# Two graph layers on one core: copies of values and transposes moved to ScalarE, the second graph's queries in seven products, and a rearranged beginning

## The chip, the cores and the metric

The kernel runs on one core of a Trainium2 chip. The core has a matrix engine (TensorE, PE in the profile, its weight loads apart as PEld), a vector engine (VectorE, DVE), a scalar engine (ScalarE, ACT), a general engine (GpSimd, POOL) and a sync engine (SP) that here only issues transfers. Each works through its own list of instructions in order and waits for the others by semaphores. The metric is the device time of one execution, in microseconds.

## What is computed

x has 16 graphs of 1024 nodes with 256 features. Both layers are residual and begin with a layer norm and a relu.

```python
h = jnp.maximum(_layernorm(x), 0.0)          # layer 0
c_adj = mean of h over its features
diff  = c_adj[:, None, :] - c_adj[:, :, None]
A     = abs(abs(sigmoid(diff) - 0.5) - 0.5) * 2.0
Wg    = adj * (A + A^T) / 2                  # one 1024 x 1024 matrix for each graph
g     = relu((h^T @ Wg) * para)              # the queries, 4 heads of 64
k, v  = h @ kv_w
x     = x + softmax(q k^T * scale) v
...
h = jnp.maximum(_layernorm(x), 0.0)          # layer 1
x = x + batchnorm(relu(batchnorm(A_hat @ h @ W1^T + b1)) @ W2^T + b2)
```

A_hat is the normalized adjacency with the identity added, the same for all graphs. All of it is float32.

## The kernel before

**Stages.** `layers` runs graph after graph. While the attention of graph b is computed, a "background" works on its neighbours: keys, values and queries of graph b+1, the second layer's aggregation and first product of graph b-1, and the norm and transposes of graph b+2. When all graphs are through, `second` does the two batch norms and the last product. A second pass (`shifted`) exists for extreme inputs and isn't entered here.

**Attention.** A unit is one graph, one pair of heads and one half of the queries; a graph has four units of four steps, and a step takes two of the eight key tiles. `scores` (L874) issues two score products per step into PSUM and two exponentials (L890, ACT). `Unit.values` (L914) multiplies the exponentials of the step before with v. `Unit.add` sums them on DVE (L909, L912), and the row sums and the outputs are folded in later (L934 to L999).

**The order of the work** is written out by hand in `attention` (L1000). In each step come, in this order: the scores and exponentials, at a "top" the transposes if one is due, the DVE sums, the value products of the step before, and then as many pieces of the background as their costs (1.71 for about 1.9 us of PE) allow against a due sum that grows evenly over the steps. `background` (L786) names the pieces; `weave` (L148) takes a piece of a main stream and then one of each side stream, from the index at which the side starts; `double` takes two of a side at once; `soon` puts an action after the next piece. Each engine executes its instructions in the order in which they were issued here, so a copy that is issued behind an exponential on the same engine waits for it.

**Around the change.**

- `transposed` (L385): for one feature half k, eight transposes on PE into two PSUM banks, and one copy for each bank into `ht` (L399, DVE). In `prepare` (L772) it is called at a top, twice for a graph.
- `keys_values` (L613): four products for the keys, each copied by ACT (L624), and then four groups for the values, `pv`, each with two copies of 128 x 256 into `v` (L641, DVE).
- `bank` (L164): PSUM tiles for all these products come from one pool of two buffers. A third product can't begin before the first has been copied out.
- `queries` (L478): the product h^T Wg in seven block products of half size instead of eight, with sums and differences of blocks on DVE (L512 among them) and two copies on ACT (L515, L516). `plain_queries` (L579): the same product in 32 tile products. In the kernel before, graphs 0 and 1 use the plain form, the others the seven products.
- `weigh` (L419): the matrix Wg in eight tiles `w`: absolute differences (L450) and a tanh (L458) on ACT, and a product with adj on DVE (L437). It reads csum as a row, `cbc`, which for all graphs but the first goes through DRAM (L414, L415). Its pieces are called slots, 17 for a graph.
- `Norm` (L298): statistics on DVE, the inverse root on POOL, the relu on ACT (L341).
- `degrees` (L224) and `graph` (L243): the node degrees, on ACT and DVE, and the combined blocks of the transposed adjacency, on POOL and by transfers issued by POOL. Both run once, in the background of graph 0.
- `aggregate` (L646): the second layer's aggregation, `pa`, in seven products; `hidden` (L721): the product with W1, `py`, whose bias is added by ACT (L737) with a column of `vec`.
- The beginning (L1082 to L1104): norm of graph 0, transposes, keys and values, weighing, plain queries, then `attention`.

Of the kernel before, what the change touches and what calls it, by code (L numbers as in the profile page):

```python
# [17 lines left out]
P = 128  # L18
# [5 lines left out]
def gnn_two_layers_kernel(  # L24
# [12 lines left out]
    nc = tc.nc  # L37
# [19 lines left out]
    neg_half = const.tile([P, NT], F32, name="neg_half")  # L57
    nc.gpsimd.memset(neg_half, -0.5)
    vec = const.tile([P, 18], F32, name="vec")
    nc.sync.dma_start(out=vec, in_=vecs)  # L60
    b1, g1, be1 = (vec[:, i * HC : (i + 1) * HC] for i in range(3))
    b2, g2, be2 = (vec[:, 3 * HC + i * CC : 3 * HC + (i + 1) * CC] for i in range(3))
    stats1 = const.tile([P, HC, B * NH, 6], F32, name="stats1")
# [32 lines left out]
    def layers(shifted):  # L96
# [73 lines left out]
                r = slice(e * HW, (e + 1) * HW)  # L170
                nc.tensor.matmul(dst[r], left[:, r], right, start=start, stop=stop)  # L171

        def load_x(b):
            xs[b] = p3.tile([P, NT, C], F32, tag="x", name=f"x_{b}")
            for half in range(2):
                t = slice(half * NT // 2, (half + 1) * NT // 2)
                nc.sync.dma_start(
                    out=xs[b][:, t], in_=x[b].rearrange("(t p) c -> p t c", p=P)[:, t]
                )
# [8 lines left out]
            )  # L188
            return t

        load_x(0)
        kvw = const.tile([P, CC, 2 * C], F32, tag="kvw", name=f"kvw_{kind}")
        nc.sync.dma_start(out=kvw, in_=kv_w.rearrange("(k p) j -> p k j", p=P))
        rows = big.tile([P, NH, NT], F32, name="rows")
# [190 lines left out]
        def transposed(b, k, halves=range(NH)):  # L385

            h = hs["a", b]
            if 0 in halves:
                ht = p3.tile([P, N], F32, tag="ht", name=f"ht_{b}_{k}")
                hts.setdefault(b, []).append(ht)  # L390
            ht = hts[b][k]
            for g in halves:
                pt = bank(f"htp_{b}_{k}_{g}")
                for j in range(FB // P):
                    t = g * (FB // P) + j
                    nc.tensor.transpose(
                        pt[:, j * P : (j + 1) * P], h[:, t, k * P : (k + 1) * P], ident
                    )
                nc.vector.tensor_copy(ht[:, g * FB : (g + 1) * FB], pt)  # L399

        def differences(b):


            cbc = p1.tile([P, N], F32, tag="cbc", name=f"cbc_{b}")
            cbcs[b] = (
                cbc.rearrange("p (t q) -> p t q", t=NT)
                if b == 0
                else cbc.rearrange("p (q t) -> p t q", t=NT)
            )
            weighers[b] = weigh(b)  # L410
            if b == 0:
                broadcast_row(cbc, columns_of(csums[b], f"c{b}"), f"c{b}")
                return
            nc.sync.dma_start(out=csum_d[b].rearrange("(p t) -> p t", p=P), in_=csums[b])  # L414
            nc.sync.dma_start(  # L415
                out=cbc, in_=csum_d[b].rearrange("(o n) -> o n", o=1).to_broadcast([P, N])
            )
# [195 lines left out]
        def keys_values(b):  # L613
            ht = hts[b]
            ks[b] = [p4.tile([P, N], F32, tag="k", name=f"k_{b}_{k}") for k in range(CC)]
            for g in range(NH):
                for j in range(CC):
                    cols = slice(g * FB, (g + 1) * FB)
                    pk = bank(f"pk_{b}_{j}_{g}")
                    for k in range(CC):  # L620
                        product(
                            pk, kvw[:, k, j * P : (j + 1) * P], ht[k][:, cols], k == 0, k == CC - 1
                        )
                    nc.scalar.copy(ks[b][j][:, cols], pk)  # L624
                    yield 1.71

            vs[b] = [p4.tile([P, NT, P], F32, tag="v", name=f"v_{b}_{k}") for k in range(CC)]
            for g in range(NT // 2):
                pv = bank(f"pv_{b}_{g}").rearrange("p (j c) -> p j c", j=2)
                for j in range(2):  # L630
                    t = 2 * g + j
                    for k in range(CC):
                        product(
                            pv[:, j, :],
                            ht[k][:, t * P : (t + 1) * P],
                            kvw[:, k, C : 2 * C],
                            k == 0,
                            k == CC - 1,
                        )
                for k in range(CC):  # L640
                    nc.vector.tensor_copy(  # L641
                        vs[b][k][:, 2 * g : 2 * g + 2, :], pv[:, :, k * P : (k + 1) * P]
                    )
                yield 1.71
# [141 lines left out]
        def background(b):  # L786

            if b == 0:
                differences(1)
                for k in range(CC):  # L790
                    yield TOP
                    transposed(1, k)
                    yield 1.0
                w, products, norm = weighers[1], keys_values(1), Norm(2, True).all()
                yield from weave(
                    islice(products, 4), (0, double(islice(w, 8))), (0, islice(norm, 4))
                )
                yield from weave(
                    plain_queries(1), (0, norm), (0, w), (5, graph()), (7, degrees())
                )  # L800
                differences(2)
                yield from islice(products, 2)
                yield from prepare(2, products)
                return
            before = hidden(b - 1)
            gather = aggregate(b - 1)
            if b + 1 < B:
                w, products, norm = weighers[b + 1], keys_values(b + 1), normed(b - 1)
                yield from weave(islice(products, 4), (0, islice(w, 4)))
                if b == 1:  # L810
                    load_later()
                yield from weave(queries(b + 1), (0, double(w)), (9, islice(norm, 5)))
                yield next(gather)
                yield from weave(products, (0, norm))
            else:
                yield from weave(endings.pop(), (2, normed(b - 1)))
                yield next(gather)
            if b + 2 < B:
                yield from weave(gather, (3, summed(b + 2)))
                yield from prepare(b + 2, before)  # L820
            elif b + 2 == B:

                yield from gather
                endings.append(before)
            else:
                yield from gather
                yield from weave(before, (0, normed_last()))
# [230 lines left out]
        with st:  # L1058
            if shifted:
                for b in range(B):  # L1060
                    if b > 0:
                        load_x(b)
                    run(Norm(b, True).all())
                    differences(b)
                    for k in range(CC):
                        transposed(b, k)
                    run(islice(weighers[b], AHEAD))
                    run(weave(plain_queries(b), (0, weighers[b])))
                    if b == 0:
                        run(degrees(), graph())  # L1070
                        load_later()
                    run(keys_values(b))
                    shifted_attention(b)
                    norm = Norm(b, False)
                    run(norm.all())
                    nc.gpsimd.dma_start(out=x1_d[b], in_=xs[b])
                    if b == B - 1:
                        attn.close()
                        turns.append(second(kind))
                    run(aggregate(b), hidden(b))  # L1080
            else:
                norm = Norm(0, True)  # L1082
                norm.stats(0, 1)
                norm.scale(0, 2)
                for t in range(2, NT, 2):
                    norm.stats(t, t + 1)
                    norm.shift(t - 2, 2)
                    norm.relu(t - 2, t - 1)
                    norm.scale(t, 2)
                norm.shift(NT - 2, 2)  # L1090
                norm.relu(NT - 2, NT - 1)
                products = keys_values(0)

                for k in range(CC):
                    transposed(0, k, (0,))
                run(islice(products, 2))
                for k in range(CC):
                    transposed(0, k, (1,))
                differences(0)
                run(weave(products, (0, islice(weighers[0], AHEAD))))  # L1100
                load_x(1)
                load_x(2)
                run(weave(plain_queries(0), (0, weighers[0]), (5, Norm(1, True).all())))
                attention()  # L1104
                attn.close()
                turns.append(second(kind))
                run(aggregate(B - 1), hidden(B - 1))
# [324 lines left out]
```

## Time and profile before

| | |
|---|---|
| median of three runs | 2658.61 us (2658.59 to 2659.17) |
| the profiled execution | 2658.52 us |
| its span in the trace | 2656.6 us |
| mean granted clock of TensorE | 0.981 |
| PE busy | 2550.8 us, 96% |
| DVE busy | 1904.3 us, 72% |
| ACT busy | 1402.4 us, 53% |
| POOL busy | 391.4 us, 15% |
| first transpose on PE | at 8.57 us |
| first scores of the attention | at 61.34 us |

The rows of the profile that belong to the two moved copies are `v<-pv` (L641, 128 copies of 418 ns) and `ht<-htp` (L399, 64 copies of 681 ns by their medians). A copy of 128 x 512 from PSUM by ACT (L624) has a median of 585 ns. A row of the timeline gives the start, the length, the engine, the line, the operation, its output and inputs, the count, and in square brackets how long the engine had been idle and what ended that. "Busy" of PE counts modelled ends of pipelined matmuls: two matmuls of half the array's width run beside each other, so that one lasts 592 ns while the group takes 0.22 us for each.

### The profile page before, as it was taken

The page shows a single profiled execution, that of the slowest core. Times are in us where ns is not written, and L with a number is a line of the kernel's source. Part 1 is how long each engine was busy: PE and PEld are TensorE (multiplying, and loading weights), DVE is VectorE, ACT ScalarE, POOL GpSimd, SP SyncE. Part 2 cuts the span into 40 slices and gives each one's busy share as a digit, 9 for nine tenths or more (in the row PEclk, how much of TensorE's full clock was granted, in tenths as well). Part 3 has the DMA queues.
Part 4 walks back from the last instruction along what each step waited for, and adds up shares of the span by engine and source line. Part 5 has one row for each costly group of instructions (what it writes and reads, how often), then busy time and mean ns, then how long its engine had stood idle before and what let it go on. Part 6 is the DMA issues. An engine that isn't in the chain of part 4 may idle for free.

```text
span 2656.6 us, 31371 instructions
## 1 busy us (share of the span) xinstructions
PE 2550.8 (96%) x11626; PEld 948.2 (36%) x11626; DVE 1904.3 (72%) x3029; ACT 1402.4 (53%) x1841; POOL 391.4 (15%) x456
## 2 busy tenths in 40 slices
PE   8999999999999999999999999999999999989995
PEld 3333333333333333333333333333333333334443
DVE  5678686868777676868677686778686776657675
ACT  5774555646373645546463736455464734335544
POOL 1640001000000001000000000010000001026653
PEclk9999999999999999999999999999999999999997
DMA  4554333142524333341525243332415242355459
GB/s 165 182 180 170 100 107 136 59 175 72 178 83 148 105 138 100 103 140 58 184 76 178 80 151 99 132 111 95 144 60 183 80 147 103 112 189 211 185 188 368
DMA packets 131041, 363.45 MB, mean 137 GB/s; under 512 B 15424, under 2 KB 32320, under 8 KB 124736
## 3 DMA queue, kind: packets, MB, share of 16 engines
q1 hardware_dynamic: 110272, 282.70, 31.4%
q0 software_dynamic: 20608, 78.66, 7.8%
q8 instruction: 94, 1.54, 0.3%
q14 instruction: 67, 0.55, 0.1%
HBM read 286.79 MB, written 74.51 MB: 136 GB/s over the span
## 4 chain that ended last, share of the span: by engine, by line
PE 63%; DVE 21%; ACT 8%; issue 3%; DMA 2%; POOL 1%; SPq 0%; POOLq 0%; DVEq 0%; ACTq 0%
PE pa L171 14%; PE sc L882 12%; PE o L923 11%; PE m_f L1227 7%; PE py L171 7%; DVE acc L912 5%; PE pk L171 4%; ACT w L450 4%; DVE w L512 3%; PE pv L171 3%; PE pg L171 2%; DMA out_dram<-xo_f 2%; DVE w L437 2%; DVE st_b L317 1%; ACT w L458 1%
## 5 line engine op out<-in xcount | busy, mean ns | idle before, releaser
L890 ACT ACTIVATE p<-sc 128x1024 f32<-128x1024 f32 x512 | 494.8, 1019 | 484.3 <-PE sc L882 483.9
L912 DVE TENSOR_TENSOR acc<-acc,p 128x1024 f32<-128x1024 f32 x384 | 471.5, 1228 | 113.5 <-ACT p L890 92.2
L882 PE MATMUL sc<-q,k 64*128 64x512 f32 x2048 | 511.6, 618 | 3.3 <-ACT p L890 3.2
L923 PE MATMUL o<-p,v 128*64 128x512 f32 x2048 | 496.6, 606 | 0.0
L171 PE MATMUL pg<-w,h_a 128*64 128x512 f32 x1600 | 358.1, 592 | 3.7 <-ACT k L624 1.9
L171 PE MATMUL pa<-aht,h_b 128*64 128x512 f32 x1536 | 344.8, 593 | 3.5 <-ACT h_b L341 3.4
L882 PEld LDWEIGHTS sc<-q,k 64*128 64x128 f32 x2048 | 177.1, 187 | 330.2 <-issue 291.7
L450 ACT ACTIVATE w<-cbc,csum 128x512 f32<-128x512 f32 x256 | 293.7, 1199 | 0.0
L171 PE MATMUL py<-at,w 128*64 128x512 f32 x1024 | 232.3, 596 | 3.6 <-DVE ht L399 3.6
L437 DVE SCALAR_TENSOR_TENSOR w<-w,adj 128x1024 f32<-128x1024 f32 x128 | 159.6, 1247 | 78.3 <-ACT w L458 74.2
L923 PEld LDWEIGHTS o<-p,v 128*64 128x64 f32 x2048 | 124.3, 136 | 251.5 <-issue 248.4
L171 PEld LDWEIGHTS pg<-w,h_a 128*64 128x64 f32 x1600 | 115.5, 137 | 231.9 <-issue 213.7
L171 PEld LDWEIGHTS pa<-aht,h_b 128*64 128x64 f32 x1536 | 110.8, 137 | 216.9 <-issue 207.2
L738 POOL DMA_DIRECT2D y_d<-y x128 | 70.5, 551 | 788.9 <-ACT y L737 781.0
L737 ACT ACTIVATE y<-py,vec 128x512 f32<-128x512 f32 x128 | 87.5, 684 | 160.0 <-PE py L171 137.4
L171 PE MATMUL pv<-kvw_f,ht 128*64 128x256 f32 x1024 | 138.2, 424 | 34.0 <-DVE v L641 34.0
L458 ACT ACTIVATE w<-w 128x1024 f32<-128x1024 f32 x128 | 135.1, 1055 | 1.8
L741 DVE BATCH_NORM_STATS2 stats<-y 128x6 f32<-128x512 f32 x128 | 85.7, 688 | 69.7 <-ACT y L737 69.6
L512 DVE TENSOR_TENSOR w<-w,w 128x1024 f32<-128x1024 f32 x112 | 132.8, 1217 | 1.5
L93 POOL TENSOR_SCALAR lnsm_b<-mv_b 128x4 f32<-128x4 f32 x32 | 12.1, 379 | 793.4 <-DVE mv_b L319 793.4
L171 PEld LDWEIGHTS py<-at,w 128*64 128x64 f32 x1024 | 73.4, 138 | 153.8 <-issue 133.7
L341 ACT ACTIVATE h_b<-x,lnsm_b 128x256 f32<-128x256 f32 x128 | 67.8, 591 | 110.7 <-DVE lnsm_b L330 110.7
(155 smaller groups left out, 2806.9 us busy)
## 6 DMA issues: line engine op xcount, KB each, us to landing
aht<-aht_d SPq DMA_DIRECT2D x224, 512.0 KB, 5.6
adj<-in_adj_dram SPq DMA_DIRECT2D x128, 512.0 KB, 4.6
y_d<-y POOLq DMA_DIRECT2D x128, 256.0 KB, 2.6
yin_f<-y_d SPq DMA_DIRECT2D x32, 1024.0 KB, 6.3
x<-in_x_dram SPq DMA_DIRECT2D x32, 512.0 KB, 5.0
para<-in_para_dram SPq DMA_DIRECT2D x64, 256.0 KB, 3.9
x_d<-x POOLq DMA_DIRECT2D x16, 1024.0 KB, 10.4
xo_f<-x_d SPq DMA_DIRECT2D x32, 512.0 KB, 8.2
```

Source lines behind the costliest of these rows:

```text
L171: nc.tensor.matmul(dst[r], left[:, r], right, start=start, stop=stop)
L437: nc.vector.scalar_tensor_tensor(w, w, 1.0, a, op0=ALU.add, op1=ALU.mult)
L450: nc.scalar.activation(w[:, t, :].rearrange("p (t q) -> p t q", q=P), cbc[:, q * NT // NH : (q + 1) * NT // NH], AF.Abs, bias=csum[:, th * ...
L458: nc.scalar.activation(made[i], made[i], AF.Tanh, scale=-0.5 / C)
L512: nc.vector.tensor_sub(block(i)[part], block(x)[part], block(y)[part])
L737: nc.scalar.activation(y, made, AF.Identity, bias=b1[:, j : j + 1])
L741: nc.vector.bn_stats(stats1[:, j, i, :], y)
L882: nc.tensor.matmul(sc[:, e, :], ks[b][k][r, m * P : (m + 1) * P], qs[b][k][r, f * FB : (f + 1) * FB], start=True, stop=True,)
L890: nc.scalar.activation(pr, sc, AF.Exp)
L912: nc.vector.tensor_add(self.acc, self.acc, pr)
L923: nc.tensor.matmul(self.o[r, :], vs[b][k][:, m, r], pr[:, e, :], start=(m == 0), stop=(m == NT - 1),)
L1227: nc.tensor.matmul(made, left[:, j, :], right[:, j, :], start=(j == 0), stop=(j == JH - 1))
```

## The change

Six edits, of which the first two act in every graph:

1. `transposed`: the copies into `ht` are made by ACT.
2. `keys_values`: the copies into `v` are made by ACT.
3. `background(0)`: graph 1's queries use `queries` in place of `plain_queries`. Two slots of the weighing follow each of the two transposes, the rest runs at two slots for a piece, and degrees and graph start at 3 and 4 instead of 7 and 5.
4. The norm of graph 1 starts at index 10 of graph 0's queries, not at 5.
5. x of graph 0 is loaded in four transfers of two tiles instead of two of four, and vec is loaded behind x and kv_w instead of first.
6. 24 transposes of the identity into an unused bank are issued on PE ahead of everything else there.

```diff
-    nc.sync.dma_start(out=vec, in_=vecs)
...
-        def load_x(b):
+        def load_x(b, parts=2):
             xs[b] = p3.tile([P, NT, C], F32, tag="x", name=f"x_{b}")
-            for half in range(2):
-                t = slice(half * NT // 2, (half + 1) * NT // 2)
+            for part in range(parts):
+                t = slice(part * NT // parts, (part + 1) * NT // parts)
...
-        load_x(0)
+        load_x(0, 4)
...
-                nc.vector.tensor_copy(ht[:, g * FB : (g + 1) * FB], pt)
+                nc.scalar.copy(ht[:, g * FB : (g + 1) * FB], pt)
...
-                    nc.vector.tensor_copy(
+                    nc.scalar.copy(
                         vs[b][k][:, 2 * g : 2 * g + 2, :], pv[:, :, k * P : (k + 1) * P]
                     )
...
                 differences(1)
+                w, products, norm = weighers[1], keys_values(1), Norm(2, True).all()
                 for k in range(CC):
                     yield TOP
                     transposed(1, k)
                     yield 1.0
-                w, products, norm = weighers[1], keys_values(1), Norm(2, True).all()
+                    yield from islice(w, 2)
                 yield from weave(
                     islice(products, 4), (0, double(islice(w, 8))), (0, islice(norm, 4))
                 )
                 yield from weave(
-                    plain_queries(1), (0, norm), (0, w), (5, graph()), (7, degrees())
+                    queries(1), (0, double(w)), (0, norm), (3, degrees()), (4, graph())
                 )
...
             else:
+                nc.sync.dma_start(out=vec, in_=vecs)
+
+                warm = bank("warm")
+                for i in range(24):
+                    j = i % (FB // P)
+                    nc.tensor.transpose(warm[:, j * P : (j + 1) * P], ident, ident)
                 norm = Norm(0, True)
...
-                run(weave(plain_queries(0), (0, weighers[0]), (5, Norm(1, True).all())))
+                run(weave(plain_queries(0), (0, weighers[0]), (10, Norm(1, True).all())))
```

## The prediction, made before the changed kernel had run

> **What bounds the kernel now.** I read the page's busy table and slices first, then the waits of TensorE, then the timeline around the wait that returns, then the same stretches with the granted clock.
>
> The busy table and the slices:
> ```profile
> PE 2550.8 (96%) x11626; PEld 948.2 (36%) x11626; DVE 1904.3 (72%) x3029; ACT 1402.4 (53%) x1841; POOL 391.4 (15%) x456
> ...
> PE   8999999999999999999999999999999999989995
> PEclk9999999999999999999999999999999999999997
> ```
> PE is busy 96% of the span, so an edit on DVE or ACT pays only where PE waits, or where the clock is lost. What PE waits for, largest first (in total, times, longest):
> ```profile
> PE pv L171 <- DVE v L641: 34.0, 14, 2.6
> ...
> PE py L171 <- DVE ht L399: 3.6, 13, 0.3
> ```
> The two largest waits that come back in every graph are exactly for the two copies that the change moves. One of them, in time order (start, length, operation, idle before):
> ```profile
> 380.12 3.62 PE L171 MATMUL pv<-kvw_f,ht 128*64 128x256 f32 x32
> 381.00 1.92 ACT L890 ACTIVATE p<-sc 128x1024 f32<-128x1024 f32 x2
> 382.97 2.54 DVE L912 TENSOR_TENSOR acc<-acc,p 128x1024 f32<-128x1024 f32 x2
> 385.44 0.75 DVE L641 COPY v<-pv 128x256 f32<-128x256 f32 x2
> 386.33 3.48 PE L171 MATMUL pv<-kvw_f,ht 128*64 128x256 f32 x16 [2.59 <-DVE v L641]
> ```
> Two banks hold products (`bank`, L164). PE filled both by 383.74. The first was complete near 382, but its copy stood on DVE behind two sums over p (L912), which waited for the exponentials on ACT. PE stood still 2.59 us, and the next 16 matmuls took 3.48 us, where 16 of the kind take 1.90 (at 393.77). Three stretches, from a table with busy times of PE, PEld, DVE, ACT, POOL and then the granted clock:
> ```profile
> 383.75:386.30 2.55, 0.00 (x0) 0.00 (x0) 2.45 (x5) 1.12 (x3) 0.00 (x0) 0.95 0.81 204
> 386.33:389.74 3.41, 3.41 (x16) 1.88 (x16) 1.12 (x3) 1.61 (x3) 0.00 (x0) 0.54 1.01 420
> 241.26:244.60 3.34, 3.34 (x24) 1.92 (x24) 1.87 (x5) 1.84 (x4) 0.00 (x0) 1.00 1.03 430
> ```
> The clock is halved for 3.41 us after the stall. This follows 12 of the 13 such stalls (386.1, 532.8 and so on to 2000.6); the one at 241 escapes.
>
> [...] the trace has 585 (ACT copies, L624). [...] the trace has one table load in all, so I charge none.
>
> **The change, part by part** (against the profiled execution, 2658.52 us: span 2656.6 and 1.9 around it; 0.1 under the median).
>
> *v copies to ACT.* In the changed program's ACT order, the first pair comes right after the two exponentials and ahead of the relus of the next pair of tiles and of the last relu of q. The exponentials end at 382.92, so the pair ends near 383.5. PE's second group ends at 383.74, so PE needn't stop. The second pair comes after two relus (1.1 us), near 385.2, and the group after next needs its bank only at 393.8 - 4.2 = 389.6. The third stands behind the last relu of q, which needs a DVE product behind the same two sums (385.5 + 0.7); it ends near 388, before the `pa` product that needs the bank (391). What ACT then has late is the next exponentials: from 388.9 in place of 386.8, read by PE a step later. I leave 0.1 us of each stall: 13 x (2.58 - 0.1) = **-32.3**. Bounds: 0 to 1 us left in each.
>
> *The clock.* Without the stall there is no half-speed stretch: 3.48 - 1.90 = 1.6 us, 12 times: **-19.2**. Bounds: none back, or all 13 us + 6.2.
>
> *ht copies to ACT.* In `prepare` (L772) the eight transposes are issued after the step's exponentials. At 306.03 they are ready by 307.1, but ACT runs the exponentials to 308.98; DVE copied at 308.53 and PE waited 0.28 (to 309.27). Now the first copy ends at 308.9 + 0.58 = 309.45 and PE starts at 309.5: 0.25 more. At the second place (316.73) exponentials end at 319.23, the copy at 319.7; PE had started at 319.50: 0.27 more. Queued behind are bias activations of y, which wait for PE over 2 us anyway. 14 graphs x 0.52 = **+7.3**. Bounds: 0 to 1.1 us a graph. DVE loses 64 x 0.68 + 128 x 0.42 = 97 us of work; off the path, worth nothing by itself.
>
> *Opening.* The input in quarters, and ahead of it no vec (0.39 us of SP issue; vec is first read in `hidden`, so it is free there): a first 256 KB should land about 1.2 us before 5.17. Eight relus at 0.585 then end near 11.2, not 12.5. But the first ht copies, on DVE at 10.87, now queue behind all eight relus: 11.7 and 12.2, against 11.6 and 12.4. Gain 0. The column copies of csum stood behind DVE's ht copies (PE waited 1.21): the second keys start near 18.8 instead of 20.30, **-1.5**. The norm of graph 1, started at 10 rather than 5, frees the q product that PE waited for at 49.17 (1.70 to about 0.6), **-1.1**, but its last relus now stand behind the q relus on ACT, and delay the first exponential (62.71): **+1.4**. The 24 transposes need only ident (ready at 1.3). At 0.105 us each warm (four in 0.42), 0.21 at half clock, they end near 6.5, ahead of the real ones (about 7.2). They could save the slow pairs at 12.52 (0.85 and 0.76 us where 0.43 is normal), 0.8 us. But the real transposes come every 0.58 us and may let the clock fall again: I take 0. Sum to 63.77: -1.2.
>
> *Graph 0's background.* This is the stretch where ACT is full:
> ```profile
> 75.00:90.00 15.00, 12.07 (x56) 3.63 (x54) 7.24 (x20) 14.60 (x16) 2.11 (x4) 1.00 0.35 108
> 90.00:103.00 13.00, 10.60 (x42) 2.99 (x38) 5.59 (x5) 13.00 (x22) 9.50 (x12) 0.87 0.51 168
> ```
> A w tile costs ACT 3.33 us (two at 1.2, one at 1.06, less overlap). Up to the exponential for the third pair of the second unit (105.67), the new order makes eight w tiles there instead of six (+6.7), four ht copies (+2.3) and two q copies (+1.1). It fills some 6.9 us that ACT idled (66.9 to 69.8, 71.75 to 75.28, less a wait near 67 for cbc, whose source is 4 us later). Laid out by hand instruction by instruction, the score that ran at 102.36 comes at 107.1, the -1.2 above included: **+4.7**. From there PE is the bound. Bounds: -1 to +8. Seven products are 4 of 32 tile products less, 16 matmuls at 0.224 (358.1/1600): **-3.6**. DVE's extra takes and sums (about 18 us) lie beside PE, as they do in every later graph. The transposed adjacency on POOL depends on POOL's own order and starts about as before (90); degrees shares its small buffer with s1 and waits for the third product, under 1 us of DVE. A clock drop follows the old wait at 95 (it is inside the 102.36); in the new order PE waits twice for ACT by over 3 us, and a drop after the second costs up to 1.6 once PE leads again: **+1.0** (0 to 3).
>
> Sum: -32.3 - 19.2 + 7.3 + 4.7 - 3.6 + 1.0 = -42.1; 2658.5 - 42.1 = 2616.4.
>
> **Rivals.**
> 1. *All cover holds.* ht costs nothing (ACT early enough) and the opening gains its 1.2: -7.3 - 5.9: 2603. For: ACT is idle half the time. Against: the exponentials end after the transposes in the trace, graph after graph.
> 2. *A new, smaller wait.* 1 us of each stall stays (+12), ht costs 1.1 a graph (+8): 2636. For: ACT serves exponentials first. Against: the 0.2 us to spare at 383.5. Near it: the clock falls for another reason and stays: 2635.
> 3. *Slower.* The exponentials ahead of the v copies end 2.5 us later than in the trace, because the ACT relus before them (379.86) wait for DVE. Then the bank comes free at 386 as now, stalls and clock drops stay, and ht (+7.3) and graph 0 (+2.1) are pure cost: 2668. It decides at 385.4 for the end of the exponentials. Against: DVE has no v or ht copy ahead of those products, so nothing makes them later.
>
> **How the numbers follow.** Forecast (2607 to 2626) 0.60; rival 1 0.17; rival 2 and the clock case 0.16; rival 3 0.05; a mixture within 0.2% (5.3 us, about what a measurement tells from no change) 0.02. Faster 0.93, same 0.02, slower 0.05. The range leaves out rival 3, the mixture and the ends of 1 and 2: 2602 to 2635.
>
> **What would show it.** Right: PE's wait at pv under 3 us in all, no half clock in the middle of the span, a period of 143.0 us from graph to graph (146.6 now, less 2.48 and 1.6, and 0.52 more), PE waiting at py for ACT ht about 14 x 0.8 us, ACT full from 75 to 106. Wrong: pv waiting for ACT v by more than 1 us each, half-clock stretches still there, or the first graph's scores (102.36) coming earlier than before.

## The result, and the profile after

The changed kernel takes 2623.9 us in the median (2623.6 to 2625.0, four runs), the kernel before in the same session 2658.6: a ratio of 0.987, 95% interval 0.9853 to 0.9887. That is 7.5 us above the 2616.4 of the prediction and inside its range. The profiled execution has a span of 2622.2 us (2656.6 before) and a mean granted clock of 0.987 (0.981).

The busy table and two rows of the slices of the changed kernel:
```profile
PE 2533.7 (97%) x11634; PEld 937.0 (36%) x11634; DVE 1844.0 (70%) x2858; ACT 1468.9 (56%) x2035; POOL 396.4 (15%) x456
...
PE   8889999999999999999999999999999999999994
PEclk9999999999999999999999999999999999999997
```
DVE lost 60 us of work and ACT gained 67. What got worse are PE's second and third digits, 9 before and 8 now. A slice is 65.6 us long, so these are 66 to 197 us, the attention of graph 0.

What PE waits for:
```profile
PE sc L882 <- ACT p L890: 13.9, 6, 4.6
PE py L170 <- ACT ht L398: 7.1, 13, 0.6
...
PE pk L170 <- ACT ht L398: 2.6, 2, 1.5
...
PE pg L170 <- DVE w L511: 1.6, 1, 1.6
```
The 34.0 us for v are gone and nothing stands in their place in the middle of the kernel. The wait for ht has doubled from 3.6 us. Scores wait 13.9 us for exponentials, all of it in graph 0.

The place at which PE stood in every graph, now at 391 us (start, length, operation, idle before):
```profile
391.07 5.35 PE L170 MATMUL pv<-kvw_f,ht 128*64 128x256 f32 x48
...
391.94 1.92 ACT L890 ACTIVATE p<-sc 128x1024 f32<-128x1024 f32 x2
...
393.75 0.65 ACT L640 COPY v<-pv 128x256 f32<-128x256 f32 x2
393.91 2.54 DVE L912 TENSOR_TENSOR acc<-acc,p 128x1024 f32<-128x1024 f32 x2
394.26 1.11 ACT L340 ACTIVATE h_b<-x,lnsm_b 128x256 f32<-128x256 f32 x2
```
The copy runs straight after the two exponentials and beside the sums, no longer behind them. All 48 products of three groups run through in one row without an idle bracket. No half-speed clock is left between 183 and 2213 us.

Time is compared best by milestones: the start of the scores of each of the 256 steps, counted from 0, changed kernel less kernel before. It is -1.83 at step 1 (63.77 us before), +3.40 at step 5 (102.36), +6.06 at step 10 (139.42), +12.26 at step 12 (152.49), **+13.21** at step 16, where graph 1's attention begins (176.20), and from there it falls by some 4 us a graph to -35.38 at step 255 (2312.14). The second stage gives 1.0 back, which is no more than its scatter: in the kernels below, which don't differ in that stage, it takes from 0.9 us less to 1.0 more than in the kernel before. So the middle brought 48.6 us and the first graph lost 13.2, of which the prediction had only about 2.1.

### The profile page after: what moved, and what is told of

It reads as the page before. It is cut to its first block, busy times and chain, and to the rows that moved or that the text cites. A ratio compares the mean times of both kernels' runs of the same rounds, so it can differ in the third digit from the quotient of the medians.

```text
span 2622.2 us, 31416 instructions
## 1 busy us (share of the span) xinstructions
PE 2533.7 (97%) x11634; PEld 937.0 (36%) x11634; DVE 1844.0 (70%) x2858; ACT 1468.9 (56%) x2035; POOL 396.4 (15%) x456
## 5 line engine op out<-in xcount | busy, mean ns | idle before, releaser
L882 PE MATMUL sc<-q,k 64*128 64x512 f32 x2048 | 513.0, 619 | 13.9 <-ACT p L890 13.9
L170 PE MATMUL pg<-w,h_a 128*64 128x512 f32 x1568 | 351.0, 592 | 4.1 <-ACT k L623 1.9
L511 DVE TENSOR_TENSOR w<-w,w 128x1024 f32<-128x1024 f32 x120 | 146.6, 1251 | 1.5
L170 PE MATMUL pk<-ht,kvw_f 128*64 128x512 f32 x512 | 117.5, 601 | 5.1 <-ACT ht L398 2.6
```

The costliest lines, as they stand in the source:

```text
L511: nc.vector.tensor_sub(block(i)[part], block(x)[part], block(y)[part])
L882: nc.tensor.matmul(sc[:, e, :], ks[b][k][r, m * P : (m + 1) * P], qs[b][k][r, f * FB : (f + 1) * FB], start=True, stop=True,)
```

## The experiments

Every kernel below was timed against the kernel before. The milestones of all of them, in us against the kernel before (whose own are in the first row):

| kernel | step 1 | step 5 | step 10 | step 12 | step 16 | step 255 | median us |
|---|---|---|---|---|---|---|---|
| before, start at | 63.77 | 102.36 | 139.42 | 152.49 | 176.20 | 2312.14 | 2658.6 |
| changed | -1.83 | +3.40 | +6.06 | +12.26 | +13.21 | -35.38 | 2623.9 |
| v alone | -0.19 | -0.20 | -0.20 | -0.20 | +2.88 | -53.15 | 2605.3 |
| first v group alone | -0.19 | -0.21 | -0.21 | -0.21 | -0.19 | -56.28 | 2602.3 |
| ht alone | +3.46 | +3.43 | +3.43 | +3.43 | +4.40 | +4.96 | 2666.9 |
| plain queries again | -1.95 | -1.95 | -1.95 | -1.95 | +2.06 | -46.41 | 2611.9 |
| no slots at transposes | -0.50 | +5.06 | +13.09 | +20.04 | +20.98 | -27.40 | 2629.6 |
| no diagonal | -1.22 | +4.44 | +4.40 | +8.30 | +9.26 | -39.18 | 2617.7 |
| no POOL arithmetic | -1.25 | +3.96 | +3.96 | +3.98 | +4.93 | -45.27 | 2614.5 |
| ht on DVE | -1.07 | +3.34 | +5.69 | +13.69 | +13.69 | -42.24 | 2615.0 |
| no idle transposes | -0.82 | +4.46 | +6.52 | +12.39 | +13.35 | -36.95 | 2623.7 |
| combined | -2.00 | -2.02 | -2.03 | -2.03 | -2.00 | -58.07 | 2600.4 |

Each row of milestones is one execution, which lay between 2.8 us below and 2.2 above the median of its kernel; and step 1 alone lies between -1.95 and -0.50 in the five kernels, the changed one among them, whose opening is the same. A difference of a microsecond or two between rows therefore shows nothing by itself.

The two theories of the gain: the bank came free too late because its copy stood behind the sums on DVE (the prediction), or DVE's total load was the trouble. Those of the loss in graph 0: the order of work on ACT, DVE's added work for the seven products, or POOL working beside DVE.

**The copies of v alone**, in the kernel before:
```diff
-                    nc.vector.tensor_copy(
+                    nc.scalar.copy(
                         vs[b][k][:, 2 * g : 2 * g + 2, :], pv[:, :, k * P : (k + 1) * P]
```


> The kernel before with the v copies on ACT and nothing else. Theory (the bank of the first value group comes free earlier, so the stall of 2.58 us goes and the half clock after it with it): the stalls at pv and the half-speed stretches from 386 to 2000 vanish, period 142.3 us instead of 146.6, about -54 us: 2604. Rival (the gain comes from less work on DVE in general, not from this place): the stall shrinks only in part and the time lies near 2630. Second rival (the clock falls for another reason): stretches stay, 2625.


Measured: 2605.3 us (2604.0 to 2608.1), ratio 0.980, interval 0.9784 to 0.9816. One line of the change brings more than all of it. It also costs something: 3.1 us between steps 14 and 16. There a pair of graph 1's own copies stands on ACT ahead of the weighing and the exponentials, and waits for its product while ACT stands idle. First this kernel, then the kernel of the next experiment, in which this pair is on DVE:
```profile
165.74 0.65 ACT L641 COPY v<-pv 128x256 f32<-128x256 f32 x2 [2.46 <-PE pv L171]
166.27 2.36 ACT L450 ACTIVATE w<-cbc,csum 128x512 f32<-128x512 f32 x2
...
172.93 2.04 PE L882 MATMUL sc<-q,k 64*128 64x512 f32 x8 [2.42 <-ACT p L890]
```
```profile
163.16 2.38 ACT L450 ACTIVATE w<-cbc,csum 128x512 f32<-128x512 f32 x2
```
The same work on ACT begins 3.1 us later, and PE waits 2.42 us for an exponential behind it.

**Only the first group's copies of v**, the ones that PE waited for:
```diff
-                    nc.vector.tensor_copy(
+                    (nc.scalar.copy if g == 0 else nc.vector.tensor_copy)(
```


> The kernel before with only the first value group's two copies on ACT, a quarter of the v copies. Theory of the bank: only the first group's copies are waited for in the middle of the graph, so nearly all of the gain of moving all of them: 2602 to 2608. Rival, relief of DVE: a quarter of that gain, about 2645.


Measured: 2602.3 us (2601.4 to 2602.9), ratio 0.9789, interval 0.9773 to 0.9805. A quarter of the copies brings the whole gain, so it isn't DVE's load but one copy's place in a queue. In the timeline of this kernel one pair is on ACT and the others, where they always were, are in time:
```profile
379.81 0.65 ACT L641 COPY v<-pv 128x256 f32<-128x256 f32 x2
379.97 2.54 DVE L912 TENSOR_TENSOR acc<-acc,p 128x1024 f32<-128x1024 f32 x2
...
383.04 1.08 DVE L641 COPY v<-pv 128x256 f32<-128x256 f32 x3
```
Its milestones fall by 56.1 us over 13 stalls: 2.80 where the clock hadn't dropped (step 22 to 23), 4.3 to 4.5 where it had.

**The copies of ht alone**, in the kernel before:
```diff
-                nc.vector.tensor_copy(ht[:, g * FB : (g + 1) * FB], pt)
+                nc.scalar.copy(ht[:, g * FB : (g + 1) * FB], pt)
```


> The kernel before with the ht copies on ACT and nothing else. Theory: each copy queues behind two exponentials; PE's wait at py for ht grows from 0.28 to 0.55 at the first place of each graph and a new 0.3 comes at the second; stalls at pv and half clock stay. +0.58 a graph, 13 or 14 times, about +8, and the opening within 1 us: 2666. Rival (relief of DVE by 43 us is worth something): no slower than before, or the stall at pv shorter.


Measured: 2666.9 us (2663.9 to 2668.1, eight runs), ratio 1.0031, interval 1.002 to 1.0041. Slower, as said; but the place was a miss: 3.46 us of it are in the opening, where the first copies queue behind the eight relus. The half clock followed only 8 of the 13 stalls in the profiled execution (2664.2 us, one of the two fastest of the eight, with a mean granted clock of 0.985 against 0.981 in the kernel before), and so hid part of the cost per graph. That the total came out near 2666 is luck: a missed cost in the opening and missing clock drops offset each other. PE's waits in this kernel:
```profile
PE pv L171 <- DVE v L641: 34.1, 14, 2.9
...
PE py L171 <- ACT ht L399: 7.0, 13, 0.5
```
The stalls at pv are as long as before, though DVE has 64 x 0.68 = 44 us less to do: again the queue, not the load.

**The old background of graph 0**, in the changed kernel:
```diff
-                    yield from islice(w, 2)
...
-                    queries(1), (0, double(w)), (0, norm), (3, degrees()), (4, graph())
+                    plain_queries(1), (0, norm), (0, w), (5, graph()), (7, degrees())
```


> The changed kernel with the background of graph 0 as it was before (plain queries for graph 1, weighing not moved ahead). Theory: that edit costs about 15 us between the third score step and graph 1's attention, the rest of the change keeps its worth: 2611, the waits of 1.65, 4.65 and 2.42 us between 140 and 180 gone. Rival (the copies on ACT, not the seven products, make graph 0 late): within 3 us of the changed kernel, 2624.


Measured: 2611.9 us (2611.4 to 2612.6), ratio 0.9825, interval 0.9809 to 0.9842. The third edit costs 12 us: the milestones are level from step 1 to step 12 at -1.95, and the 4.0 lost between step 12 and 16 are what "v alone" (3.1) and "ht alone" (1.0) lose there as well. The waits of 1.65 and 4.65 us are gone. The one of 2.42 is not, against the expectation: it stands at 171 us, as in "v alone", and belongs to the copies.

**The two slots after each transpose taken out**, the seven products kept:
```diff
                     yield 1.0
-                    yield from islice(w, 2)
```


> The changed kernel without the two weighing slots that follow each transpose of graph 1 (all of that tile's work returns to the products). Theory (the w tile that is put ahead of the first key copy on ACT makes the keys late by one tile's 3.1 us): the fourth score step, at 86.57 in the changed kernel, comes at 83.5; what DVE loses later stays: 2621. Rival (the slots fill idle time of ACT and help): the step stays near 86.6 or the total grows by up to 4: 2627.


Measured: 2629.6 us (2625.9 to 2630.2), ratio 0.9889, interval 0.9872 to 0.9905. The theory's step 3 came true (the scores came 3.0 us earlier against this kernel's own opening), its total did not: by step 5 the work was back, and at step 16 this kernel is 7.8 us behind the changed one. Work that ACT is spared early comes due later, at the seven products that need the tiles. So the slots at the transposes aren't what costs the 11 us; without them it is more. Part of the 7.8 is the clock's: between 106 and 168 us this execution has 17.1 us at half clock, the changed kernel has 3.4.

**Without the diagonal in the degrees** (eight products with the identity and eight reductions on DVE are left out, the diagonal is set to zero):
```diff
+            nc.gpsimd.memset(diag, 0.0)
...
-                db = p1.tile([P, P], F32, tag="s1", name=f"db_{t}")
-                nc.vector.tensor_mul(db, blk, ident)
-                nc.vector.tensor_reduce(diag[:, t : t + 1], db, AX.X, ALU.add)
```


> The changed kernel with the eight products with the identity and eight reductions of degrees left out (16 DVE instructions, 7.7 us between 115 and 147; the diagonal is set to zero, so the degrees count it twice). Theory (DVE is full from 105 to 150 and sets the pace there): the waits of 1.65 and 4.65 us and the clock drop after them go or shrink to under 2 us together, 2615. Rival (ACT's waits for the transfers of adj_t set the pace): ACT still waits some 7 us at 126 and the time stays above 2620.


Measured: 2617.7 us (2616.3 to 2619.0), ratio 0.9847, interval 0.983 to 0.9863; 4.0 us less at step 16. The wait of 1.65 us is gone, that of 4.65 is down to 2.21: somewhat less than the theory said. ACT still waits for adj_t, but at most 1.3 us at a time, and the rival's 2620 isn't reached. The 16 instructions are 7.6 us of DVE in the changed kernel. They are not new, the kernel before spends 5.4 us on them; but they start at 115 us instead of 126 and fall among the seven products. The prediction had under 1 us for this.

**Without POOL's arithmetic in `graph`** (the sums and differences of blocks of the transposed adjacency and the addition of the identity are left out, the transfers stay, and raw blocks are aggregated):
```diff
...
-                    if part == t * P // HB:
-                        blk = a[:, n, n, t * P % HB : t * P % HB + P]
-                        nc.gpsimd.tensor_add(blk, blk, ident)
...
-                sub = nc.gpsimd.tensor_sub
-                sub(two[:, 0], b12, a[:, 0, 0])
-                sub(two[:, 1], b22, two[:, 0])
...
-                sub(b12, b22, b12)
-                sub(one, b21, two[:, 1])
+                two, one = a[:, 0], a[:, 1, 0]
```


> The changed kernel with the additions and subtractions of graph() on POOL left out; its transfers stay, and carry uncombined blocks, so the second layer aggregates something else. Theory (POOL's work stretches DVE's instructions beside it, 8.8 us in all between 90 and 165, and DVE is full there): DVE's instructions take their usual time and the delay of the seven products shrinks by half or more: 2614 to 2618. Rival (the instruction count of DVE alone is too much): within 2 us of the changed kernel.


Measured: 2614.5 us (2612.9 to 2616.0), ratio 0.9838, interval 0.9822 to 0.9855; 8.3 us less at step 16, and no wait of PE for DVE or ACT between 140 and 160. Not an instruction of DVE was taken away. What got shorter are DVE's instructions themselves. The takes of the seven products, w<-w,w, between 90 and 165 us (shortest, median, longest in ns, first and last start); first the changed kernel, then this one:
```profile
L511 DVE TENSOR_TENSOR w<-w,w x8: 1212/1746/2909, 99.8 to 142.1; 128x1024 f32<-128x1024 f32 x8
```
```profile
L500 DVE TENSOR_TENSOR w<-w,w x8: 1216/1218/1220, 100.3 to 135.2; 128x1024 f32<-128x1024 f32 x8
```
And how full the engines are from 120 to 135 us (busy PE, PEld, DVE, ACT, POOL, then the clock), in the kernel before, the changed one, and this one:
```profile
120.00:135.00 15.00, 15.00 (x70) 5.07 (x68) 10.95 (x16) 6.78 (x11) 13.71 (x19) 1.00 0.97 338
```
```profile
120.00:135.00 15.00, 14.71 (x66) 4.89 (x66) 14.59 (x20) 6.75 (x12) 14.82 (x18) 1.00 0.81 286
```
```profile
120.00:135.00 15.00, 15.00 (x72) 5.22 (x68) 14.55 (x25) 7.69 (x11) 3.47 (x5) 1.00 0.86 302
```
The busy time of DVE in the last two is the same, but in this kernel it holds 25 instructions (of mixed sizes), in the changed one 20. A busy time alone doesn't show that an engine is being held up.

**The copies of ht back on DVE**, all else as changed:
```diff
-                nc.scalar.copy(ht[:, g * FB : (g + 1) * FB], pt)
+                nc.vector.tensor_copy(ht[:, g * FB : (g + 1) * FB], pt)
```


> The changed kernel with the ht copies back on DVE. Theory: the wait at py returns from 0.55 to 0.28 and the new 0.3 at the second place goes, 13 times 0.58 = -7.5, and the first keys of the opening start about 1 us earlier, the copies for graph 2 about 2 us: 2614. Rival (ACT's copies only fill idle time): within 2 us of the changed kernel.


Measured: 2615.0 us (2610.5 to 2617.2), ratio 0.9833, interval 0.9816 to 0.9849. The wait at py is back to 3.6 us in total; each graph after the first is 0.6 us faster, the first one no faster.

**Without the 24 idle transposes**, all else as changed:
```diff
-                warm = bank("warm")
-                for i in range(24):
-                    j = i % (FB // P)
-                    nc.tensor.transpose(warm[:, j * P : (j + 1) * P], ident, ident)
```


> The changed kernel without the 24 idle transposes of the identity at the beginning; all else as in it. Theory: they gain nothing, because the clock after them is at half speed again from 8.5 to 15.3 us in the changed kernel's trace (the real transposes come one every 0.58 us and leave TensorE idle for a third to a half of that). So the first scores come within 0.7 us of 58.34, and the total within 1.5 us of the changed kernel's 2623.9. Rival: they save the slow pairs of transposes (about 0.8 us) and move the first scores; then this kernel's first scores come at 59.1 or later and the total is 2624.7 or more.


Measured: 2623.7 us (2621.9 to 2624.9), ratio 0.9871, interval 0.9854 to 0.9889: no different. The opening doesn't speak so clearly. First the changed kernel, then this one:
```profile
1.39 4.62 PE L1087 MATMUL warm<-ident 128*128 128x128 f32 x24 [1.39 <-POOL ident masks.py:199]
7.09 0.33 PE L395 MATMUL htp<-ident,h_a 128*128 128x128 f32 x1 [1.08 <-ACT h_a L340]
7.67 0.33 PE L395 MATMUL htp<-ident,h_a 128*128 128x128 f32 x1 [0.26 <-ACT h_a L340]
...
11.65 5.46 PE L170 MATMUL pk<-ht,kvw_f 128*64 128x512 f32 x16 [1.48 <-ACT ht L398]
```
```profile
11.55 6.32 PE L170 MATMUL pk<-ht,kvw_f 128*64 128x512 f32 x16 [1.47 <-ACT ht L398]
```
The real transposes come one every 0.58 us, and PE is idle 0.26 of it; before the first of them it had stood for 1.08 us. With the idle transposes the clock still fell, at 8.5, and stayed at half until 15.3. Here the pairs of products start 0.85 us apart until about 16.9, where 0.43 is normal, and the first scores come 1.0 later, as the rival had it. But the same opening with the idle transposes took 5.31, 5.52, 5.84 and 6.56 us for those 16 products in four of the other kernels: 6.32 lies within the spread. If they gain something at the opening, it is no more than that spread, and by step 16 nothing of it is left (13.21 and 13.35).

**Combined**: the changed opening without the idle transposes, the old background, ht on DVE, and the first group of v alone on ACT (the edits shown above, joined).


> What the runs so far favour, put together: of the changed kernel the opening (input in quarters, vec later, norm of graph 1 at index 10), but no idle transposes; graph 0's background as before the change (plain queries, transposes without slots between them); the copies into ht on DVE as before; and of the four groups of v only the first one's two copies on ACT. Theory (gains add up): the kernel before with only the first group's copies on ACT ran in 2602.3; the earlier input, worth 1.8 us at the second step of the scores, is kept up to graph 1's attention, because with the plain queries DVE has slack between 105 and 150 us: 2600.5, within 2. Rival (the early part is bound by a later wait, which takes the opening's gain back): 2602.3 or more, with the start of graph 1's attention no earlier than in that kernel (176.0).


Measured: 2600.4 us (2599.4 to 2601.1), ratio 0.9782, interval 0.9766 to 0.9799. The intervals of this and of "first v group alone" overlap, but their four runs each do not (2601.4 to 2602.9 there), and the milestones agree: 2.00 us are gained by step 1 and are still there at step 16, and -58.07 stands against -56.28 at step 255. The first key products now follow the transposes at once:
```profile
7.01 3.08 PE L395 MATMUL htp<-ident,h_a 128*128 128x128 f32 x8 [7.01 <-ACT h_a L340]
10.05 5.23 PE L170 MATMUL pk<-ht,kvw_f 128*64 128x512 f32 x16
...
17.83 1.06 PE L211 MATMUL cbp_c<-ident,cb_c 128*128 128x128 f32 x8 [1.21 <-DVE cb_c L200]
```
With ht on ACT they began at 11.6 behind a wait of 1.5, as the prediction had laid out ("behind all eight relus: 11.7"). Little of these 1.5 us arrives at the attention: with ht on DVE, PE waits 1.21 us for the columns of csum, which it doesn't with ht on ACT, and step 1 comes at -2.00 here and at -1.95 in "plain queries again". The input in quarters, the later vec and the later norm of graph 1 were not taken apart.

## Why the prediction was right, and where it failed

Its sum and what the traces show, in us:

| term of the prediction | predicted | measured |
|---|---|---|
| v stalls and clock drops | -32.3 - 19.2 = -51.5 | -56.1 |
| ht on ACT, middle | +7.3 | 13 x 0.58 = +7.5 |
| opening and graph 0 up to step 5 | +4.7 | +3.4 |
| from there to graph 1's attention | -3.6 + 1.0 = -2.6 | +9.8 |
| second stage | 0 | +1.0 |
| sum | -42.1 | -34.4 |

*v copies and clock: right, a little small.* The mechanism is shown by the first two experiments and by the timeline at 391. That a pair of copies takes 0.6 us on ACT (from 382.92 to near 383.5) was an estimate; the pair at 393.75 took 0.65. Of the missing 4.6 us, 1.3 are the 0.1 that I left in each stall, of which nothing is left. Another 2.1 come from reading the gap: the row at 386.33 has 2.59 of idle, but counted from start to start PE is 2.75 late there, 0.16 more. These products are recorded as 0.38 us long, and without a stall the next pair starts 0.22 after the one before, so neighbours overlap by 0.16 in the records, which a gap from an end to a start leaves out. No run here shows how much of the 0.16 is true overlap and how much comes from the modelled ends, and a count from start to start needs neither. The last 1.2 are not placed. The period from graph to graph is 142.84 us, where the prediction had 143.0.

*ht: right in the middle* (0.27 and 0.32 a graph for 0.25 and 0.27, over 13 graphs, not 14). The wait at py that it named as a sign, 14 x 0.8 us, was too large: it is 7.1 us in 13 waits. That the copies eat the earlier input was right for the first keys. The 3.46 of "ht alone" show what the same copies cost in the old opening, where the first products of the keys start at 13.11 in place of 11.61 and 16 of them take 6.57 us in place of 4.83: a price that the working never set against the edit by itself.

*Opening and the stretch where ACT is full: right.* First scores came at 58.34 and step 1 at 61.94, though one term was off: the second keys start at 19.71, not near 18.8. ACT is full where it was said to be:
```profile
75.00:90.00 15.00, 10.58 (x48) 3.02 (x46) 8.37 (x22) 14.87 (x17) 1.25 (x2) 1.00 0.54 157
90.00:106.00 16.00, 11.33 (x44) 3.50 (x42) 11.32 (x11) 15.90 (x26) 11.81 (x14) 0.89 0.44 140
```
From step 1 to 5 it cost 5.2, where the working had 5.9. (The pieces that the working names, 6.7 + 2.3 + 1.1 - 6.9, make only 3.2; the rest lay in the layout by hand, which it doesn't show.)

*The steps that failed* lie between step 5 and step 16, where +9.8 stands against -2.6. Of these 12.4 us, 4.0 are the copies of graph 1's values and graph 2's transposes on ACT between steps 12 and 16: the prediction counted ACT up to 106 us and the stalls in the middle, and put these at nothing. "v alone" loses 3.1 there, "ht alone" 1.0, "plain queries again" 4.0. The larger step, the other 8.4, is "DVE's extra takes and sums (about 18 us) lie beside PE, as they do in every later graph", with "under 1 us of DVE" for degrees and "From there PE is the bound". From 106 to about 155 us DVE is the bound, and PE stands behind it. PE's gaps over 1 us in graph 0's attention from there on, from the timeline of the changed kernel:
```profile
143.61 1.94 PE L170 MATMUL pg<-w,h_a 128*64 128x512 f32 x8 [1.65 <-DVE w L511]
...
155.71 3.44 PE L882 MATMUL sc<-q,k 64*128 64x512 f32 x8 [4.65 <-ACT p L890]
...
178.14 2.90 PE L882 MATMUL sc<-q,k 64*128 64x512 f32 x8 [2.42 <-ACT p L890]
```
The last is the wait of 2.42 us behind the v copies, which is there in every kernel with all v copies on ACT, whether DVE is full or not. The largest is put down to ACT, but ACT was idle. Its rows ahead of it:
```profile
152.98 0.63 ACT L499 ACTIVATE q<-q 128x512 f32<-128x512 f32 x1 [9.38 <-DVE q L497]
...
154.65 1.92 ACT L890 ACTIVATE p<-sc 128x1024 f32<-128x1024 f32 x2
```
ACT waited 9.38 us for DVE's q, and the exponentials stood behind that relu in its order: DVE, then ACT, then PE.

Why is DVE late here and in no later graph? Because graph 0 alone has `graph` and `degrees` in its background. From 105 to 150 us DVE is busy for 44.1 of 45 us; in the kernel before it was 37.4. Two things fill it. One is more work at that time: the seven products' sums and takes, less the copies that went to ACT, and the diagonal, which now starts 11 us earlier. The other was there before and had been hidden by DVE's idle time: instructions that POOL holds up. Taken over 90 to 165 us, the durations of all DVE instructions sum to 59.6 us in the kernel before and 70.6 in the changed one, and what they have above the median of their own row in the whole kernel is 8.8 and 10.0 of that. Without POOL's arithmetic it is 0.0. The 10.0 is somewhat low, because all eight products with the identity run beside POOL and raise their own median: they take 5.3 us together, and 2.3 without POOL's arithmetic.

The lengths of single instructions show it as well. In the changed kernel a take lasts 1.22 us in the median of the whole kernel, but 1.75 in the median and 2.91 at most between 90 and 165 us, where POOL is busy for 68.9 of 75 us; without POOL's arithmetic it lasts 1.22 there too. The 10.0 us lie, to within 0.1, in instructions with two inputs in SBUF; those with one input (acc<-acc, 0.70 us) or with one in PSUM (q<-pg,q, 0.68 us) keep their time. Why the ones are hit and the others not, no run here shows. The kernel before shows it too, and the prediction overlooked it, because it read busy shares of that stretch and no durations. There, the products with adj between 98 and 124 us (a mean of 1247 ns in the kernel as a whole):
```profile
L437 DVE SCALAR_TENSOR_TENSOR w<-w,adj x4: 1473/1896/2920, 98.0 to 123.7; 128x1024 f32<-128x1024 f32 x4
```

What each part costs can't be added up: taking out the diagonal saves 4.0 us at step 16, POOL's arithmetic 8.3, and the seven products with their order 11.2, with the same slack behind all three. Without POOL's arithmetic, step 5 to step 16 costs +1.0 us, and the forecast of -2.6 with the 4.0 of the copies would make +1.4. That the three meet is shown; how the 11.2 divides without the others is not, and the earlier start of `degrees` and `graph`, which is part of the edit, was not tried by itself.

*The rivals.* Cover didn't all hold (ht's 7.5), and no new wait came at pv. The slower rival needed exponentials ending after 385.4; at the same place they end at 393.86, which is 382.9 in the time of the kernel before (the changed one is 10.95 us later there), as the prediction had it. The clock's own return was right, but 155 and 179 us have half clocks that the kernel before hadn't, both after waits in graph 0.

*Luck.* The copies brought 4.6 us more than forecast and the opening with graph 0's first steps 1.3. Without these the total would have been near 2630, outside the range. So the mechanism of the gain was right, but that the sum held is owed in part to errors of opposite sign.

## What to carry to other kernels

When a bank is released late, look at which copy is late and behind what it stands in its engine's order, and move that one alone: here two copies of eight gave 56 us, and the other six, with the transposes' copies, only cost. Before work is put on an engine "beside PE", compare the durations of its instructions in that stretch with those of the same row elsewhere, since a high busy share may be instructions that are being held up (here 14.59 of 15 us with 20 instructions, and 14.55 with 25 without POOL's arithmetic), and ask what runs there once only. A wait for ACT with ACT idle just before it belongs to whatever ACT was waiting for.

## What was not expected of the hardware

- A stall of 2.6 us costs 2.8 by the starts of the instructions and, where the clock fell, another 1.6; but the clock did not fall after each. In the trace of the kernel before, the stretches at half clock start at whole multiples of 3.41 us from one another (386.07, 532.84 and 679.62 are 43 of them apart). Laid on that grid, each of the 12 stalls that the half clock followed has between 2.32 and 2.60 us in one stretch of 3.41, and the clock fell at the end of that stretch. The stall before 241.26 lies across two, with 0.61 and 1.96 us, and the clock stayed. Counted from the span's start, the grid of the changed kernel lies 1.3 us off that of the kernel before. So that the clock fell after 12 of 13 stalls in one execution and after 8 in that of "ht alone" need not come from the edit; for "ht alone" it was not shown.
- Idle time isn't all that counts. In the kernel before, the clock fell at 2618.39 after a stretch of 3.41 us in which PE stood still for 1.71 in all, less than the 1.96 at 241. In the changed kernel it fell at 8.5 although 24 transposes had run without a break until 6.0 and PE stood still for only 1.6 of the 3.41 us before, 1.08 of it ahead of the first real transpose and the rest between the next ones. What else counts there is open.
